# A 4-row transpose of softmax weights, widened to a transpose of a whole 128x128 tile that is zero but for those rows

## Chip, cores and metric

The kernel runs on one core of one Trainium2 chip. The metric is device time in microseconds; lower is better. Three runs of the kernel before gave 2450.37, 2450.66 and 2451.76 us, so the median is 2450.66 us. A profile of a further execution, with a record for every instruction, is what "the profile" and "the trace" mean below.

## The reference

There are 128 graphs of 128 nodes with 512 features each, and a weighted 128x128 adjacency matrix per graph, all in float32. Four layers follow one another, each of the form x = layernorm(x + layer(x, adj)). Layers 0, 2 and 3 multiply by a normalised adjacency and by weights. The change lies in layer 1, cut here to what matters:

```python
def _L1_gnn_ref(x, adj_matrix, W_qk, W_v):
    qk = jnp.einsum('bnd,ed->bne', x, W_qk)
    q, k = jnp.split(qk, 2, axis=-1)
    v = jnp.einsum('bnd,ed->bne', x, W_v)
    inv_scale = 1.0 / ATT_DIM ** 0.5
    scores = jnp.einsum('bnd,bmd->bnm', q, k) * inv_scale
    w = jnp.sum(scores * adj_matrix, axis=-1, keepdims=True)
    w = jax.nn.softmax(w, axis=1)
    return w * v
```

So each graph has one number w per node; these 128 numbers go through a softmax over the nodes, and row n of v is scaled by the weight of node n.

## The kernel before, in words

**Tiling.** The work is cut into 32 tiles of 4 graphs (G = 4, NT = 32). Nodes lie on the 128 partitions. A tile's features are a 128x4x512 array in SBUF (`x`), and everything of the four layers happens to it on chip. The tiles are staggered: in the loop at the end of the kernel function, one pass works on layers 0 and 1 of tile t and on layers 2 and 3 of tile u = t - 1, so that the matmuls of one can be placed among those of the other.

**Matmuls.** The layers' weight products use a 2x2 block scheme with seven products (B11, T1, B21, B22, T2, T3, T4), in `project` (line 526) for layers 0, 2 and 3 and in `l1_out` (line 729) for layer 1. Their results are the PSUM tiles `p_o` and `p_v` of the profile. A matmul of two float32 operands shows as two records in the trace; a transpose shows as one. Products of `project` take hooks: functions that are called after the product named, so that their TensorE instructions stand at that place in TensorE's order. GpSimd forms the sums of left operands (`agg3s` and the like), ScalarE copies PSUM to SBUF and normalises, VectorE adds results and takes the statistics.

**Softmax of layer 1.** `l1_scores` (line 695) leaves `w`, 128 nodes by 4 graphs. `l1_softmax` (line 716) transposes it on TensorE to 4 rows of 128 (PSUM tile `p_w`), takes each row's minimum on VectorE (the sign is turned, so this is the maximum of the scores), has ScalarE form the exponentials `e` with their sum, and has VectorE scale `e` in place by the reciprocal of the sum. `e` is a tile of 4 partitions by 128, of a tag with one buffer. `l1_add` (line 775) transposes `e` back to 128 nodes by 4 graphs on TensorE (PSUM tile `p_ws`), has VectorE copy that to `ws`, and then adds `v` scaled by `ws` to `x`. In TensorE's order `p_w` comes after product B11 of layer 3 of the tile before, and `p_ws` after its product B21 (line 903), so that four matmuls of B11, one transpose, four of T1, four of B21, the other transpose and four of T2 follow one another; in the trace, each four are eight records.

A TensorE transpose is a matmul whose stationary operand is the data and whose moving operand is the identity. The shapes in the profile name both: in `4*128 4x4`, the data has 4 rows and 128 columns and the identity is 4x4.

**What sets the order.** Every instruction is first recorded in a plan (class `Plan`, line 127). TensorE keeps the order in which the program recorded it. The other engines' instructions are ordered by a list scheduler (`schedule`, line 197): each has an estimated duration (`estimate`, line 292) and a due time worked back from those that need it. For a transpose on TensorE the estimate is

```python
max(109, 0.85 * n) if method == "transpose"
```

with n the number of elements of the output per partition. `emit` (line 268) then issues all instructions, which is why nearly every row of the profile names line 271; the tiles tell them apart. The PSUM tiles `p_w`, `p_ws`, `p_agg` and `p_xT` share a pool of three banks (`ps_t`, line 339) in turn. Constants such as `ident` (the identity) and `nhalf` (line 388) are made once at the start, from a pool of their own.

Of the kernel before, what the change touches and what calls it, by code (L numbers as in the profile page):

```python
# [10 lines left out]
FP = mybir.dt.float32  # L11
# [4 lines left out]
P = 128  # L16
K = 32
Q = P // K
G = 4
# [292 lines left out]
def kernel(  # L312
# [13 lines left out]
    nc = Plan(tc.nc, estimate)  # L326
# [4 lines left out]
    const = Pool(nc, ctx.enter_context(tc.tile_pool(name="const", bufs=1)), 1)  # L331
# [3 lines left out]
    sp = Pool(nc, ctx.enter_context(tc.tile_pool(name="sp", bufs=4)), 4)  # L335
# [7 lines left out]
    st = {}  # L343
# [15 lines left out]
    def weight(src, name, queue, turned=False):  # L359


        w = const.tile([P, 2, 7, H], FP, tag=name, name=name)
        for h in range(2):
            to = w[:, :, 2 * h:2 * h + 2].rearrange("p c j m -> p c (j m)")
            if turned:
                for b in range(Q):
                    queue.dma_start(to[b * K:(b + 1) * K], src.rearrange("(b h c k) m -> h b k c m", b=Q, h=2, c=2)[h][b])
            else:
                queue.dma_start(to, src.rearrange("(h c p) m -> h p c m", h=2, c=2)[h])
        return w  # L370
# [7 lines left out]
    def broadcast_row(src, name, queue):  # L378
        r = const.tile([P, F], FP, tag=name, name=name)
        queue.dma_start(r, bass.AP(tensor=src.tensor, offset=src.offset, ap=[[0, P], [1, F]]))  # L380
        return r

    ident = const.tile([P, P], FP, tag="ident", name="ident")
    make_identity(tc.nc, ident.real())
    p = ps_t.tile([P, C, P], FP, tag="pt", name="p_warm")
    for _ in range(WARM):
        nc.tensor.transpose(p[:, 0], ident, ident)
    nhalf = const.tile([P, G], FP, tag="nhalf", name="nhalf")
    nc.vector.memset(nhalf, -0.5)
    w0_sb = weight(w0, "w0_sb", nc.sync)  # L390
    b0_sb = broadcast_row(b0, "b0_sb", nc.sync)
    wqk_sb = tp.tile([P, C, 2 * ATT], FP, tag="row", name="wqk_sb", bufs=1)
# [233 lines left out]
    def norm_stats(name, t, r, pairs):  # L626
        if name == "o3" and (t, r, pairs[-1]) != (last, 1, 1):
            return norm_last(name, t, r, pairs)
        z = st["x", t]
        qs = slice(pairs[0], pairs[-1] + 1)  # L630
        mv = sp.tile([P, 2, 2], FP, tag="mv", name=f"mv{name}_{t}_{r}")
        for q in pairs:
            n = 2 if name == "o3" else 1
            s = sp.tile([P, n, 6], FP, tag="bn", name=f"bn{name}_{t}_{r}_{q}")
            for h in reversed(range(n)):
                nc.vector.bn_stats(s[:, h], z[:, 2 * q + r, h * (F // n):(h + 1) * (F // n)])
            nc.vector.bn_aggr(mv[:, q, :], s)
        rstd = sp.tile([P, 2], FP, tag="rstd", name=f"rstd{name}_{t}_{r}")
        mr = sp.tile([P, 2], FP, tag="mr", name=f"mr{name}_{t}_{r}")
        nmr = sp.tile([P, 2], FP, tag="nmr", name=f"nmr{name}_{t}_{r}")  # L640
        nc.gpsimd.tensor_scalar(rstd[:, qs], mv[:, qs, 1], LN_EPS, None, ALU.add)
        nc.gpsimd.tensor_tensor(rstd[:, qs], rstd[:, qs], nhalf[:, qs], ALU.pow)
        if name == "o3":
            zg = z[:, G - 1]
            nc.vector.tensor_scalar(zg, zg, mv[:, 1, 0:1], rstd[:, 1:2], ALU.subtract, ALU.mult)
            nc.sync.dma_start(out[B - 1], zg)
            return
        nc.gpsimd.tensor_tensor(mr[:, qs], mv[:, qs, 0], rstd[:, qs], ALU.mult)
        nc.scalar.mul(nmr[:, qs], mr[:, qs], -1.0)
        for q in pairs:  # L650
            zg = z[:, 2 * q + r, :]
            nc.scalar.activation(zg, zg, AF.Identity, bias=nmr[:, q:q + 1], scale=rstd[:, q:q + 1])
# [63 lines left out]
    def l1_softmax(t):  # L716
        p = ps_t.tile([P, P], FP, tag="pt", name=f"p_w_{t}")
        nc.tensor.transpose(p[:G, :], st.pop(("w", t)), ident)
        mn = sp.tile([G, 1], FP, tag="mn", name=f"mn_{t}")
        nc.vector.tensor_reduce(mn, p[:G, :], AX.X, ALU.min)  # L720
        e = sp.tile([G, P], FP, tag="e", name=f"e_{t}", bufs=1)
        ssum = sp.tile([G, 1], FP, tag="ssum", name=f"ssum_{t}")
        nc.scalar.activation(e, p[:G, :], AF.Exp, bias=mn, scale=-1.0, accum_out=ssum)
        rsum = sp.tile([G, 1], FP, tag="rsum", name=f"rsum_{t}")
        nc.vector.reciprocal(rsum, ssum)
        nc.vector.tensor_scalar(e, e, rsum, None, ALU.mult)
        st["e", t] = e

    def l1_out(t, hooks):

# [44 lines left out]
    def l1_add(t):  # L775

        p = ps_t.tile([P, P], FP, tag="pt", name=f"p_ws_{t}")
        nc.tensor.transpose(p[:, :G], st.pop(("e", t)), ident[:G, :G])
        ws = sp.tile([P, G], FP, tag="ws", name=f"ws_{t}")
        nc.vector.tensor_copy(ws, p[:, :G])  # L780
        for r in range(2):
            for g in (r, 2 + r):
                for h in range(2):
                    zg = st["x", t][:, g, h * H:(h + 1) * H]
                    nc.vector.scalar_tensor_tensor(zg, st["v", t][r, h][:, g // 2, 0:H], ws[:, g:g + 1], zg,
                                                   ALU.mult, ALU.add)
            norm_stats("v", t, r, (0, 1))
# [68 lines left out]
    def begin():  # L856

        prep_rows(0)
        prep_transpose(0)
        weight_sums(w0_sb, nc.vector)  # L860
        l0_agg(0, nc.vector, ONE_BY_ONE)
        prep_rows(1)
        l0_out(0, {B11: [lambda: prep_transpose(1)], B22: [lambda: l0_agg(1)]})
        weight_sums(wv_sb, nc.vector)
        for w in (w2x_sb, w2a_sb, w3_sb):
            weight_sums(w, nc.gpsimd)

        l0_out(1)
        l1_turn(0, turn_on_tensor, (0,))
        finish_tails()  # L870
        l1_turn(0, turn_on_tensor, (1,))
        l1_out(0, {T3: [lambda: l1_turn(1, turn_on_tensor)]})
        l1_out(1, {B11: [lambda: l1_scores(0)], T1: [lambda: l1_softmax(0)], B21: [lambda: l1_add(0)]})
        l2_both(0, 0)
        l2_out(0, {B11: [lambda: l2_both(0, 1), lambda: prep(2)], T1: [lambda: l1_scores(1)], T2: [lambda: l1_softmax(1)], T3: [lambda: l1_add(1)]})
        l0_agg(2)
        l2_turn(1)
        l0_out(2, {B21: [lambda: l2_agg(1, 0)], T1: [lambda: l2_agg(1, 1)]})
        l3_agg(0)
        l3_bias(0)  # L880
        l3_out(0)
# [8 lines left out]
    for t in range(2, NT):  # L890
        u = t - 1
        if t > 2:
            l0_out(t, {T1: [lambda: l2_agg(u, 0)], T2: [lambda: l2_agg(u, 1)]})
        tails.append(lambda: l1_turn(t))
        prep(t + 1)
        l2_out(u)
        if t < last:
            l0_agg(t + 1)
        l1_out(t, {})
        l3_agg(u)  # L900
        l1_scores(t)
        l3_bias(u)
        l3_out(u, {B11: [lambda: l1_softmax(t)], B21: [lambda: l1_add(t)]})
        if t < last:
            l2_turn(t)
# [43 lines left out]
```

## Time and profile before

| What | us |
|---|---|
| Median of three runs | 2450.66 |
| The profiled execution, its own time | 2451.53 |
| Its span, first to last instruction | 2449.8 |
| TensorE matmuls busy | 2437.9 |
| TensorE weight loads busy | 2087.3 |
| VectorE busy | 1714.5 |
| GpSimd busy | 1316.0 |
| ScalarE busy | 996.4 |

The mean granted TensorE clock of that execution is 0.999 of full speed. In the profile, PE is TensorE's matmuls, PEld its weight loads (they run beside the matmuls), DVE is VectorE, ACT is ScalarE, POOL is GpSimd and SP issues most DMAs. A row of groups reads: line, engine, operation, output<-inputs, shapes, count | busy time in us, mean ns of one | idle time of the engine just ahead of them, and what ended it. A row of the timeline reads: start in us, length in us, engine, line, operation, output<-inputs, shapes, count; instructions of one kind in succession are merged. Matmuls are pipelined, and the end of a record is modelled, so records overlap. "issue" means that the engine waited for nothing that the profile shows.

### The profile page before, as it was taken

To read this page: it belongs to the slowest core of one execution; us is meant where nothing else is said; L and a number is where in the kernel's file an instruction comes from. 1 tells how busy PE (TensorE), PEld (TensorE's weight loads), DVE (VectorE), ACT (ScalarE), POOL (GpSimd) and SP (SyncE) were. 2 spreads that over 40 slices of the span, in tenths; PEclk is the share of its full clock that TensorE was granted. 3 is DMA by queue.
4 is the path that set the end of the run, shared out by engine and by line. 5 is a ranking of instruction groups with operands and counts; after the bars stand their busy time and mean duration, and the time that the engine had idled before them with its cause. 6 is when DMAs were issued, how large, how long until landed. Compare 5 with 4: busy or idle time off the path is not lost.

```text
span 2449.8 us, 35470 instructions
## 1 busy us (share of the span) xinstructions
PE 2437.9 (100%) x12462; PEld 2087.3 (85%) x12462; DVE 1714.5 (70%) x3396; ACT 996.4 (41%) x2117; POOL 1316.0 (54%) x1580
## 2 busy tenths in 40 slices
PE   9999999999999999999999999999999999999998
PEld 7888888888888888888888888888888888888887
DVE  7767766677666777766776667766677676777666
ACT  4334343443434444344443444333444334443345
POOL 6464555555555555555455554645546455555543
PEclk9999999999999999999999999999999999999999
DMA  5133233442424423244332443234442333423220
GB/s 181 48 99 104 73 108 91 125 125 57 116 78 125 125 69 109 78 121 125 84 93 82 117 125 104 73 99 104 120 125 61 96 102 117 125 74 96 67 80 35
DMA packets 393266, 241.15 MB, mean 98 GB/s; under 512 B 140416, under 2 KB 358016, under 8 KB 393088
## 3 DMA queue, kind: packets, MB, share of 16 engines
q1 hardware_dynamic: 393088, 238.88, 35.4%
q8 instruction: 99, 1.62, 0.3%
q14 instruction: 79, 0.65, 0.1%
HBM read 126.62 MB, written 112.20 MB: 97 GB/s over the span
## 4 chain that ended last, share of the span: by engine, by line
PE 96%; DMA 1%; DVE 1%; POOL 1%; SPq 0%; issue 0%; ACT 0%; POOLq 0%; DVEq 0%
PE p_o L271 61%; PE p_v L271 20%; PE p_agg L271 14%; PE p_sc L271 1%; SPq L271 0%; DMA x<-in_x_dram 0%; PE p_w L271 0%; DVE x L271 0%; DMA xT1s<-x 0%; DVE u_o L271 0%; PE p_ws L271 0%; DMA xT1y<-xT1s 0%; PE p_xT L271 0%; POOL xT2s L271 0%; DMA xT2y<-xT2s 0%
## 5 line engine op out<-in xcount | busy, mean ns | idle before, releaser
L271 PE MATMUL p_o<-w_sb,agg 128*128 128x256 f32 x2048 | 471.3, 380 | 0.9 <-DVE u_o L271 0.9
L271 PEld LDWEIGHTS p_o<-w_sb,agg 128*128 128x128 f32 x2048 | 386.1, 190 | 52.8 <-DVE u_o L271 0.9
L271 ACT COPY agg<-p_agg 128x512 f32<-128x512 f32 (+1 forms) x415 | 226.3, 553 | 406.0 <-PE p_agg L271 405.8
L271 PE MATMUL p_v<-wv_sb,xT 128*128 128x320 f32 x1024 | 291.7, 433 | 0.1
L271 PE MATMUL p_o<-w2x_sb,xT 128*128 128x256 f32 x1024 | 263.0, 379 | 1.0 <-ACT xT L271 1.0
L271 DVE TENSOR_TENSOR v<-p_v,v 128x320 f32<-128x320 f32 x316 | 154.5, 490 | 155.4 <-PE p_v L271 154.8
L271 PE MATMUL p_o<-w2a_sb,agg 128*128 128x256 f32 x1024 | 262.8, 379 | 0.0
L271 PEld LDWEIGHTS p_v<-wv_sb,xT 128*128 128x128 f32 x1024 | 191.9, 190 | 76.7 <-ACT xT L271 0.6
L271 PEld LDWEIGHTS p_agg<-anT,x 128*128 128x128 f32 x2048 | 238.7, 192 | 7.0 <-DVE anT L271 0.5
L271 DVE TENSOR_TENSOR u_o<-p_o,u_o 128x512 f32<-128x512 f32 (+1 forms) x196 | 129.1, 671 | 160.6 <-PE p_o L271 159.1
L271 PE MATMUL p_agg<-anT,x 128*128 128x128 f32 x2048 | 239.4, 275 | 0.3 <-DVE anT L271 0.3
L271 PEld LDWEIGHTS p_o<-w2x_sb,xT 128*128 128x128 f32 x1024 | 194.2, 190 | 30.8 <-ACT xT L271 1.4
L271 PE MATMUL p_v<-wv_sb,xT1s 128*128 128x320 f32 x768 | 217.6, 433 | 0.8 <-POOL xT1s L271 0.6
L271 PEld LDWEIGHTS p_o<-w2a_sb,agg 128*128 128x128 f32 x1024 | 194.6, 190 | 26.4
L271 POOL TENSOR_SCALAR rstdo<-mvo 128x2 f32<-128x2 f32 (+1 forms) x131 | 35.7, 272 | 320.9 <-DVE mvo L271 318.3
L271 PE MATMUL p_o<-w2x_sb,xT2s 128*128 128x256 f32 x768 | 197.2, 379 | 0.0
L271 PE MATMUL p_o<-w2a_sb,agg2s 128*128 128x256 f32 x768 | 197.1, 379 | 0.0
L271 ACT ACTIVATE x<-x,nmro,rstdo 128x512 f32<-128x512 f32 x256 | 195.0, 808 | 3.4
L271 PEld LDWEIGHTS p_v<-wv_sb,xT1s 128*128 128x128 f32 x768 | 145.5, 190 | 59.0 <-POOL xT1s L271 2.0
L271 PE MATMUL p_o<-w_sb,agg0s 128*128 128x256 f32 x768 | 181.1, 379 | 0.4 <-DVE u_o L271 0.4
L271 PE MATMUL p_o<-w_sb,agg3s 128*128 128x256 f32 x744 | 173.8, 383 | 0.0
L271 DVE BATCH_NORM_STATS2 bno<-x 128x6 f32<-128x512 f32 x258 | 170.4, 682 | 3.9
(146 smaller groups left out, 4255.8 us busy)
## 6 DMA issues: line engine op xcount, KB each, us to landing
x<-in_x_dram SPq DMA_DIRECT2D x31, 1024.0 KB, 6.5
out_dram<-x SPq DMA_DIRECT2D x31, 1024.0 KB, 5.4
xT2s<-x SPq DMA_DIRECT2D x120, 256.0 KB, 2.8
xT2y<-xT2s SPq DMA_DIRECT2D x240, 128.0 KB, 2.7
xT1s<-x SPq DMA_DIRECT2D x120, 256.0 KB, 2.5
xT1y<-xT1s SPq DMA_DIRECT2D x240, 128.0 KB, 3.1
sa<-ana SPq DMA_DIRECT2D x120, 128.0 KB, 3.2
ya<-sa SPq DMA_DIRECT2D x120, 128.0 KB, 3.3
```

Source lines behind the costliest of these rows:

```text
L271: getattr(getattr(self.nc, op.engine), method)(*[v.real() if isinstance(v, Ref) else v for v in args], **{k: v.real() if isinstance(v, Ref ...
```

## The change

A constant tile `e_sb` of 128x128 is made at the start and filled with zeros by VectorE. In `l1_softmax`, `e` is no longer a tile of its own but rows 0 to 3 of `e_sb`; the exponentials are written and scaled there, and rows 4 to 127 stay zero. In `l1_add`, the transpose takes the whole of `e_sb` as data and the whole identity, and writes all 128 columns of `p_ws`. Columns 0 to 3 hold what they held before, and only those are copied to `ws`; columns 4 to 127 are zeros that nobody reads.

```diff
+    e_sb = const.tile([P, P], FP, tag="e_sb", name="e_sb")
+    nc.vector.memset(e_sb, 0.0)
...
-        e = sp.tile([G, P], FP, tag="e", name=f"e_{t}", bufs=1)
+        e = e_sb[:G, :]
...
-        st["e", t] = e
...
-        nc.tensor.transpose(p[:, :G], st.pop(("e", t)), ident[:G, :G])
+        nc.tensor.transpose(p, e_sb, ident)
```

## The prediction

> **What bounds the kernel now.** I read the page first: busy shares, then the chain of work that ended last.
>
> ```profile
> span 2449.8 us, 35470 instructions
> PE 2437.9 (100%) x12462; PEld 2087.3 (85%) x12462; DVE 1714.5 (70%) x3396; ACT 996.4 (41%) x2117; POOL 1316.0 (54%) x1580
> ...
> PE 96%; DMA 1%; DVE 1%; POOL 1%; SPq 0%; issue 0%; ACT 0%; POOLq 0%; DVEq 0%
> ```
>
> TensorE is busy for the whole span and is 96% of the chain, so a nanosecond of TensorE time is a nanosecond of the kernel, and nothing else counts unless it makes TensorE wait. But a busy PE hides what a matmul really costs: the records overlap, since each is drawn longer than the distance to the next. The cost must be read from start to start. Next I took the small transposes by tile, among the groups with shapes kept apart (matmuls, then weight loads).
>
> ```profile
> L271 PE MATMUL p_w<-ident,w 128*4 128x128 f32 x32 | 8.6, 270 | 0.1
> L271 PE MATMUL p_ws<-ident,e 4*128 4x4 f32 x32 | 7.0, 220 | 0.0
> ...
> L271 PEld LDWEIGHTS p_ws<-ident,e 4*128 4x128 f32 x32 | 4.3, 133 | 10.7 <-issue 10.7
> ```
>
> p_ws is the transpose that the change edits: 32 of them, one per tile, 0.22 us each, and 10.7 us of weight-load idle that no semaphore explains (0.33 each). Last, TensorE alone in time, in the last tile but for its end:
>
> ```profile
> 2383.65 0.59 PE L271 MATMUL p_o<-w_sb,agg 128*128 128x256 f32 x2
> 2384.08 0.27 PE L271 MATMUL p_w<-ident,w 128*4 128x128 f32 x1
> 2384.19 1.89 PE L271 MATMUL p_o<-w_sb,agg3s 128*128 128x256 f32 x8
> 2385.92 1.89 PE L271 MATMUL p_o<-w_sb,agg 128*128 128x256 f32 x8
> 2387.74 0.22 PE L271 MATMUL p_ws<-ident,e 4*128 4x4 f32 x1
> 2387.89 3.29 PE L271 MATMUL p_o<-w_sb,agg3s 128*128 128x256 f32 x14
> ```
>
> One p_o record is 0.38 us; eight in a row take 1.89, so their starts lie (1.89 - 0.38) / 7 = 0.216 apart. The last of the eight before p_ws thus starts at 2385.92 + 7 x 0.216 = 2387.43. From there: p_ws starts 0.31 later (0.216 is the streaming of that p_o; 0.094 is idle array), the next p_o starts 0.15 after p_ws, and the 14 that follow take 3.29 where 13 x 0.216 + 0.38 = 3.19: another 0.10 at the first of them. Taking p_ws out would leave one step of 0.216, so it costs 0.310 + 0.150 + 0.104 - 0.216 = 0.348 us. (The third decimal is from the starts in the trace; all 32 p_ws show it within 2 ns, also the two with other neighbours.) The same view gives the price of p_w, a transpose that streams 128 columns from all 128 rows: it starts 2384.08 - (2383.65 + 0.59 - 0.38) = 0.22 after the p_o before it, the next p_o starts 0.11 later, and that one's eight take 1.89, so no gap on either side. It costs 0.109 us.
>
> **What the Trainium skill says.** "TensorEngine Tiling (Array Packing)", section Key Properties, says that changing the tiling mode drains TensorE; its list of configurations has modes of 32 rows, which is what a 4-row operand would fit. The trace agrees in kind: p_ws, the only matmul with fewer than 128 rows, is the only one with a gap on both sides, and p_w, with 4 columns but all rows, has none where its operand is ready. "TensorE: Matmul & The Clock Gate", section Step-by-step, says that the next tile's weights load while this one's matmul runs, pulled ahead where row groups do not conflict or the load goes to the background buffer. The trace agrees: the load of a p_o starts with the matmul before it, that of p_ws only at 2387.74, with its own matmul. The same page's LDWEIGHTS section says that load time goes by columns, not rows: 133 ns for the 4-row load, 141 for a 128-row one (p_xT), so the full tile loads about as fast.
>
> **The change part by part.** The instruction lists of the two kernels, compared engine by engine with numbers and line shifts taken off, have the same order. The planner's estimate for a transpose is max(109, 0.85 x columns), which is 109 for 4 and for 128, so no due time moves; only the points below differ.
>
> 1. p_ws from 4 to 128 rows (both operands) and from 4 to 128 streamed columns. The nearest rows are p_w (128 rows, 128 columns, 0.109) and p_xT (128x128 weights too; eight in a row take 1.04 with a record of 0.272, so (1.04 - 0.272) / 7 = 0.110 each). I take 0.109. Saved: 0.348 - 0.109 = 0.239 per tile, x 32 = 7.65 us, all on the bounding engine. Bounds: if only one of the two gaps goes, about 0.1 less per tile (4.4 us left); if neither goes, see the slower rival.
>
> 2. The e that p_ws waits for. In every other tile the scaling of e ends late. At 1860.51 it lasts 1.10, end 1861.61; the last p_o before that p_ws starts at 1860.19 + 7 x 0.216 = 1861.70. From DVE's end to TensorE's load the trace shows 0.11 (p_w waits so: last DVE end 1933.84, load 1933.95). So the load of e, now free to run under that p_o, starts at 1861.72 and has until 1861.92. It needs 0.11 at the steady pace, 0.19 as the longest record: just covered. I take 0; if the cover fails, up to 0.1 in 14 tiles, 1.4 us. A gain is excluded, as nobody waits for e alone.
>
> 3. 31 matmuls (p_agg of layer 2, two p_xT) now also wait for TensorE's own semaphore, since p_ws fills as much of the bank as its successor in it. The p_ws meant is 18 lines of the list back, some 12 us, so the count is long reached. A semaphore instruction takes 51 ns on TensorE's queue, which runs ahead: p_agg rows with such waits show 0.0 idle. I take 0; bound 31 x 0.05 = 1.6 us; no gain.
>
> 4. The memset of e_sb, once, on DVE: the nearest row is GpSimd's memset of the same size, 0.20 us. After its first memset (end 0.85) DVE sits idle for 2.73 us until adj lands at 3.58. Cost 0; uncovered, 0.2 us once.
>
> 5. e shares one buffer over tiles as before (a tag with one buffer), so Exp waits for no one new; Exp, reduce and scaling have the same 4x128 shape.
>
> What is late next when TensorE runs 0.239 ahead? After p_ws it needs GpSimd's agg3s (done before p_ws) and DVE's reads of two regions. DVE sits idle 0.31 us for TensorE at 1864.19 in that tile, 0.65 in the neighbour (1939.82): more than 0.239, so DVE moves along with TensorE and each later wait keeps its distance. p_w's own wait (0.145 in 28 tiles) is behind DVE's queue, and that queue too is tied to TensorE by then; it stays.
>
> Sum: span 2449.8 - 7.65 = 2442.1. That execution took 2451.53, which is 1.73 outside the span: 2443.9 for its like. The median of the runs shown, 2450.66, lies 0.87 below that execution, so I forecast 2450.66 - 7.65 = 2443.0.
>
> **The rivals.**
> A. Part of it comes back: the load of e is late in every other tile (1.4 us), or the semaphore waits show (1.6), or one of both gaps stays. For it: a cover of only 0.1 us. Against: no p_agg is late now with two waits. With the first two, 2446.0; 2444.5 with one.
> B. The gaps come from the hand-over (a wait on two semaphores in mid-stream), not from the rows: the change does nothing for them, and streaming is free under them: 2450.7. Against: p_w has the same two waits, and at 2384.08 no gap.
> C. Slower. The gaps stay, and the stream now has 128 columns in place of 4: 0.109 x 124 / 128 = 0.105 more per tile, x 32 = 3.4 us: 2454.0. The place is p_ws on TensorE; it decides if p_ws still starts 0.31 after the p_o before it. For it: the stationary operand still has 128 columns and the change widens all else. Against: p_xT, of the very shape, follows others at 0.109 with no gap.
>
> **How the numbers follow.** Forecast case (2442.2 to 2444.0) 0.80; A 0.11, which ends at 2446.2 with both waits shown in full; B 0.05; C 0.04. The bound of what can be told from no change is 0.2%, 4.9 us, that is 2445.8: A lies mostly under it. Faster 0.89, same 0.07, slower 0.04. The range runs from 2442.0 (half the spread of the three runs under the forecast case) to 2446.2; it leaves out B and C, 0.09.
>
> **What would show it.** p_ws as 128*128 128x128, near 272 ns, its load near 141 and without the idle for issue; the start of p_ws 0.216 after the p_o before, the next p_o 0.11 after it, and eight p_o in 1.89 behind that. Memset of e_sb before 1.2 us; chain still 96% PE; span near 2442. Wrong, if p_ws starts 0.31 after its p_o (C or B), if "DVE e" appears ahead of p_ws among the waits (A), or if TensorE's gaps are gone and the span is not shorter: then DVE held TensorE elsewhere.

## The result and the profile after

The changed kernel takes 2445.07 us (median of 10 runs, 2443.5 to 2446.01), the kernel before 2451.32 (10 runs, 2450.37 to 2452.36). The ratio is 0.9973, with a 95% interval of 0.9965 to 0.9981: faster by 4.7 to 8.6 us, 6.25 between the medians. A second measurement, among the experiments, gave 7.45.

The page of the changed kernel has the same picture as before: span, busy time by engine, and the chain by engine.

```profile
span 2443.3 us, 35474 instructions
...
PE 2430.7 (99%) x12462; PEld 2088.2 (85%) x12462; DVE 1714.2 (70%) x3397; ACT 996.3 (41%) x2117; POOL 1318.7 (54%) x1580
...
PE 97%; DVE 1%; POOL 0%; DMA 0%; issue 0%; ACT 0%; SPq 0%; POOLq 0%; DVEq 0%
```

The small transposes among the changed kernel's groups, matmuls and then the weight load:

```profile
L271 PE MATMUL p_ws<-ident,e_sb 128*128 128x128 f32 x32 | 8.7, 272 | 0.0
...
L271 PEld LDWEIGHTS p_ws<-ident,e_sb 128*128 128x128 f32 x32 | 4.5, 140 | 1.3
```

The records of p_ws have become longer in sum, 8.7 us of matmul for 7.0 and 4.5 of loads for 4.3, and the kernel is faster. What went is the idle of the load for "issue", 10.7 us before and not in the row now. TensorE in time, in the last tile but for its end, shows it from start to start:

```profile
2377.66 0.27 PE L271 MATMUL p_w<-ident,w 128*4 128x128 f32 x1
2377.76 1.89 PE L271 MATMUL p_o<-w_sb,agg3s 128*128 128x256 f32 x8
2379.49 1.89 PE L271 MATMUL p_o<-w_sb,agg 128*128 128x256 f32 x8
2381.22 0.27 PE L271 MATMUL p_ws<-ident,e_sb 128*128 128x128 f32 x1
2381.33 3.19 PE L271 MATMUL p_o<-w_sb,agg3s 128*128 128x256 f32 x14
```

The last of the eight p_o before p_ws starts at 2379.49 + 7 x 0.216 = 2381.00. p_ws starts 0.22 later, the next p_o 0.11 after that, and its fourteen take 3.19, which is 13 x 0.216 + 0.38 with nothing over. All three gaps are gone. By the starts in the trace, all 32 p_ws cost 0.111 us or within 2 ns of it (two have other neighbours), against 0.348 before: 0.237 saved per tile, 7.6 us in all.

The weight loads around p_ws show what the gaps are made of. Before:

```profile
2387.74 0.13 PEld L271 LDWEIGHTS p_ws<-ident,e 4*128 4x128 f32 x1 [0.33 <-issue]
2387.89 0.30 PEld L271 LDWEIGHTS p_o<-w_sb,agg3s 128*128 128x128 f32 x2
```

and in the changed kernel:

```profile
2381.01 0.14 PEld L271 LDWEIGHTS p_ws<-ident,e_sb 128*128 128x128 f32 x1
2381.22 0.30 PEld L271 LDWEIGHTS p_o<-w_sb,agg3s 128*128 128x128 f32 x2
```

Before, the load of p_ws and that of the p_o behind it begin with their own matmuls (2387.74 and 2387.89). In the changed kernel they begin 0.21 and 0.11 ahead of them, under the matmul before. The second p_o load follows the first by 0.11, since one lasts 0.19 and the two together 0.30; the gap of 0.104 behind p_ws is of that size. So of the 0.348, only the 0.094 ahead is a wait before anything of p_ws begins, and much of the rest is two loads that no matmul covers.

This execution's span is shorter by 6.5, not by 7.6. The rest lies in the first 24 us. TensorE there, before:

```profile
1.34 5.74 PE L271 MATMUL p_warm<-ident 128*128 128x128 f32 x30 [1.34 <-POOL ident masks.py:199]
...
20.36 1.99 PE L271 MATMUL p_o<-w_sb,agg0s 128*128 128x256 f32 x8 [0.35 <-DVE u_o L271]
22.19 2.06 PE L271 MATMUL p_agg<-anT,x 128*128 128x128 f32 x17
```

and in the changed kernel:

```profile
1.35 6.20 PE L271 MATMUL p_warm<-ident 128*128 128x128 f32 x30 [1.35 <-POOL ident masks.py:199]
...
21.38 1.99 PE L271 MATMUL p_o<-w_sb,agg0s 128*128 128x256 f32 x8 [0.81 <-DVE u_o L271]
23.21 1.05 PE L271 MATMUL p_agg<-anT,x 128*128 128x128 f32 x8
```

The warm-up transposes, the same 30 in both, took 0.46 us longer, and by 23 us the kernel is 1.0 late. By the starts in the traces, p_warm goes at first at 0.213 us from start to start and then at 0.109; the pace changes after 21 steps before and after 26 in the changed kernel, which accounts for the 0.46. Another 0.46 is the longer wait of p_o for u_o. Whether the new memset does that is the first question for the experiments.

### The profile page after: what moved, and what is told of

It reads as the page before. It is cut to its first block, busy times and chain, and to the rows that moved or that the text cites. A ratio compares the mean times of both kernels' runs of the same rounds, so it can differ in the third digit from the quotient of the medians.

```text
span 2443.3 us, 35474 instructions
## 1 busy us (share of the span) xinstructions
PE 2430.7 (99%) x12462; PEld 2088.2 (85%) x12462; DVE 1714.2 (70%) x3397; ACT 996.3 (41%) x2117; POOL 1318.7 (54%) x1580
## 4 chain that ended last, share of the span: by engine, by line
PE 97%; DVE 1%; POOL 0%; DMA 0%; issue 0%; ACT 0%; SPq 0%; POOLq 0%; DVEq 0%
PE p_o L271 62%; PE p_v L271 20%; PE p_agg L271 14%; PE p_sc L271 1%; DMA ana<-in_adj_dram 0%; PE p_w L271 0%; DVE x L271 0%; DVE u_o L271 0%; PE p_xT L271 0%; PE p_ws L271 0%; DVE w_sb L271 0%; DVE ana L271 0%; DVE agg0s L271 0%; POOL rstdo L271 0%; POOL w2x_sb L271 0%
```

## The experiments

The theory: a matmul with few rows among matmuls of 128 rows empties TensorE on both sides, so rows are what counts. The rivals: the stream of 4 columns is too short to cover the weight loads; or the transpose mode does it. The two other transposes vary rows and columns together; the three matmuls vary them one at a time. By the traces, p_ws has the same two semaphore waits in all of these kernels, so the hand-over, rival B of the prediction, is no difference between them. In the table, the steps are ns from start to start as most tiles have them: into p_ws, between its two records where it has two, from p_ws to the next p_o, and from that p_o to its successor. The cost is their sum less two steps of 216. The last columns hold 32 times the cost less that of the kernel before, and what was measured.

| p_ws | rows x streamed columns | steps | cost, us | worked out, us | measured, us |
|---|---|---|---|---|---|
| before, transpose | 4 x 4 | 310, 150, 320 | 0.348 | - | - |
| rows64, transpose | 64 x 64 | 310, 202, 320 | 0.400 | +1.7 | +1.75 |
| rows96, transpose | 96 x 96 | 216, 87, 242 | 0.113 | -7.5 | -6.86 |
| changed, transpose | 128 x 128 | 216, 109, 218 | 0.111 | -7.6 | -6.25, -7.45 |
| mm_r4c4, matmul | 4 x 4 | 309, 132, 178, 320 | 0.507 | +5.1 | +5.63 |
| mm_r4c128, matmul | 4 x 128 | 309, 213, 200, 320 | 0.610 | +8.4 | +8.98 |
| mm_r128c4, matmul | 128 x 4 | 216, 28, 112, 299 | 0.223 | -4.0 | -3.67 |

Every measured value lies above the one worked out, by 0.1 to 1.3 us, and each interval (1.6 to 3.8 us either way) covers the one worked out. A small cost that these kernels share, outside p_ws, is thus neither shown nor excluded.

**The memset alone.** The kernel before, with this added:

```diff
+    e_sb = const.tile([P, P], FP, tag="e_sb", name="e_sb")
+    nc.vector.memset(e_sb, 0.0)
```

> The kernel before with only the memset of a 128x128 tile of zeros added at the start; e and its transpose stay 4 rows. Theory (the 1.1 us that the changed kernel lost in its first 24 us is chance of the start, a later grant of the clock): time within 0.7 us of the kernel before, p_ws at 0.31 / 0.15 / 0.10 as before. Rival (the memset, or what moves in SBUF with it, delays the start): about 1.1 us slower, with the wait of p_o for DVE u_o near 20 us at 0.8 in place of 0.35.

2451.55 us beside 2451.70 for the kernel before, ratio 0.9999 (0.9991 to 1.0008); the gaps at p_ws are there. The memset in its trace, by tile (count, then min, median and max in ns):

```profile
L271 DVE MEMSET e_sb<- x1: 165/165/165, 0.8 to 0.8; 128x128 f32 x1
```

TensorE in time has the wait that the rival named, but not the delay:

```profile
20.66 1.99 PE L271 MATMUL p_o<-w_sb,agg0s 128*128 128x256 f32 x8 [0.80 <-DVE u_o L271]
22.49 1.72 PE L271 MATMUL p_agg<-anT,x 128*128 128x128 f32 x14
```

p_agg starts at 22.49: 0.3 after the kernel before, 0.7 ahead of the changed one. So in this execution the memset brings a third of the loss at most; the interval of the time, 2 us either way, is too wide to tell 1.1. That called for the kernel before, profiled again.

> The kernel before, profiled once more, for its first 24 us. Theory (the start varies by chance): the second block of p_o from agg0s, which started at 20.36 in its first profile and between 20.47 and 21.38 in kernels with the memset, starts 0.1 us or more off 20.36. Rival (the memset sets it): again at 20.36 within 0.05, with a wait of 0.35.

```profile
20.01 1.99 PE L271 MATMUL p_o<-w_sb,agg0s 128*128 128x256 f32 x8 [0.35 <-DVE u_o L271]
21.84 2.39 PE L271 MATMUL p_agg<-anT,x 128*128 128x128 f32 x20
```

The same program is 0.35 earlier at this place than in its first profile, with the wait the rival named and the start that it did not. The pace of p_warm changes after 16 steps here, where it was 21. The span is 2449.8 all the same. So a start early by a third of a microsecond is chance and need not reach the end. The expectation left out two kernels with the memset: in rows64 and in the version called later, both below, this block starts at 20.36 and 19.86. Over ten profiles with the memset it starts between 19.86 and 21.38, and over two without it at 20.01 and 20.36. The ranges overlap; a share of the memset of a few tenths of a microsecond remains open.

**The changed kernel once more,** unaltered, beside the others:

> The changed kernel itself once more, beside the others. Theory (all 7.6 us that the trace shows at p_ws are gained; the first measurement's 6.25 fell short by chance of the start): ratio near 0.9969, 7 to 8 us faster than before. Rival (about 1.3 us are given back in every run): ratio near 0.9974, 6.0 to 6.5 us faster.

2444.42 us beside 2451.87: 7.45 faster, ratio 0.9971 (0.9959 to 0.9982), span 2442.6. TensorE in time, where it was 1.0 late in its first profile:

```profile
20.47 1.99 PE L271 MATMUL p_o<-w_sb,agg0s 128*128 128x256 f32 x8 [0.57 <-DVE u_o L271]
```

The same program starts this block 0.91 earlier than in its first profile, and the pace of p_warm changes after 16 steps in place of 26. So the late start belongs to that one execution, not to the change. At p_ws the steps are the same in both profiles. The interval covers both expectations, and the median sides with the first. That all of the first ten executions fell short by chance of the start is not shown, as only one of them was profiled.

**Rows.** In place of the whole tile:

```diff
-        nc.tensor.transpose(p, e_sb, ident)
+        nc.tensor.transpose(p[:, :64], e_sb[:64], ident[:64, :64])
```

> The changed kernel, but the transpose takes 64 rows of e_sb and a 64x64 identity, so p_ws has 64*128 64x64. Theory (fewer rows than the whole array put TensorE into another tiling, with an idle array on both sides): p_ws again starts 0.31 after the p_o before it, costs 0.35 to 0.40, the time is that of the kernel before, 0 to +1.7 us. Rival (it was the short stream of 4 columns that could not cover the loads): the gaps are gone or half gone, p_ws costs about 0.11 to 0.2, 5 to 7 us faster than before.

2453.45 us beside 2451.70, ratio 1.0008 (0.9999 to 1.0016). TensorE in time, last tile but for its end:

```profile
2387.25 1.89 PE L271 MATMUL p_o<-w_sb,agg 128*128 128x256 f32 x8
2389.07 0.27 PE L271 MATMUL p_ws<-ident,e_sb 64*128 64x64 f32 x1
2389.27 3.07 PE L271 MATMUL p_o<-w_sb,agg3s 128*128 128x256 f32 x13
```

2389.07 is 0.31 after the last p_o's start (2387.25 + 7 x 0.216 = 2388.76): the gap of 4 rows, unchanged with 64 rows and a stream sixteen times as long. The step after it grew by 52 ns. Next, the same edit with 96:

> The changed kernel, but the transpose takes 96 rows of e_sb and a 96x96 identity: p_ws is 96*128 96x96. Theory (a matmul of 96 rows already has the whole array, as the skill's list of tilings ends at 64 rows): no gaps, p_ws costs about 0.11, 7 to 8 us faster than before. Rival (every matmul with fewer than 128 rows has the gaps): p_ws starts 0.31 after the p_o before it and costs 0.40 to 0.43, 1.6 to 2.6 us slower.

2445.01 us beside 2451.87, ratio 0.9972 (0.9961 to 0.9982).

```profile
2379.45 1.89 PE L271 MATMUL p_o<-w_sb,agg 128*128 128x256 f32 x8
2381.18 0.25 PE L271 MATMUL p_ws<-ident,e_sb 96*128 96x96 f32 x1
2381.27 3.00 PE L271 MATMUL p_o<-w_sb,agg3s 128*128 128x256 f32 x13
```

No gap ahead: 2381.18 is 0.22 after the start before it. The edge lies between 64 and 96 rows, and "fewer than 128" is ruled out. The change needed no more than 96 rows.

**Stream and mode.** The transpose as an ordinary float32 matmul, which is two records, with its estimate in the plan held at 109 so that the order of all instructions stays:

```diff
-        nc.tensor.transpose(p, e_sb, ident)
+        nc.tensor.matmul(p[:, :G], e_sb[:G], ident[:G, :G], start=True, stop=True)
```

> The changed kernel, but p_ws is an ordinary float32 matmul of 4 rows of e_sb with a 4x4 identity (two records in place of one); its estimate in the plan is held at 109, so the order is unchanged. Base for the two like it. Theory (rows): gaps as before ahead of the first and behind the second record, cost about 0.35 plus a second load of 0.11 to 0.15, so 0.46 to 0.5 per tile, 3.5 to 5 us slower than before. Rival (it is the transpose mode with 4 rows that drains): no gap of 0.31, cost about 0.22, 4 us faster than before.

2457.33 us beside 2451.70, ratio 1.0023 (1.0013 to 1.0033): 5.6 us slower at a cost of 0.507, both a little above what the theory expected.

```profile
2391.63 1.89 PE L271 MATMUL p_o<-w_sb,agg 128*128 128x256 f32 x8
2393.45 0.38 PE L271 MATMUL p_ws<-ident,e_sb 4*128 4x4 f32 x2
2393.76 3.07 PE L271 MATMUL p_o<-w_sb,agg3s 128*128 128x256 f32 x13
```

The gap of 0.31 is there without the transpose mode. With all rows, `e_sb` and `ident[:, :G]`:

> As the ordinary matmul of 4 rows, but with all 128 rows of e_sb and 4 columns of the identity, so 128*128 128x4: only the rows differ. Theory (rows): no gap ahead of it, only the loads show: 0.11 for each of two records, 0.22 per tile, 4 us faster than before. Rival (the short stream): the cost of the 4-row matmul, 0.46 to 0.5, 3.5 to 5 us slower than before.

2448.03 us beside 2451.70, ratio 0.9985 (0.9978 to 0.9991).

```profile
2382.06 1.89 PE L271 MATMUL p_o<-w_sb,agg 128*128 128x256 f32 x8
2383.79 0.28 PE L271 MATMUL p_ws<-ident,e_sb 128*128 128x4 f32 x2
2383.93 3.05 PE L271 MATMUL p_o<-w_sb,agg3s 128*128 128x256 f32 x13
```

The stream is as short as before and the gap is gone (2383.79 is 0.22 after 2383.57). What a short stream does cost shows here alone: the steps 28, 112 and 299 are two loads of about 0.11 that 4 columns do not cover, 0.223 in sum. And with 4 rows but all columns, `e_sb[:G]` and `ident[:G, :]`:

> The ordinary matmul of 4 rows, but with 128 columns of the identity streamed in place of 4: only the length of the stream differs. Theory (rows): the gap of 0.31 ahead and 0.10 behind stay, and two streams of 128 columns come on top of the cost of 0.507 that the 4-column one showed: 0.6 to 0.72 per tile, 8 to 12 us slower than before. Rival (a long stream covers the loads and the gaps): about 0.22 per tile, 4 us faster than before.

2460.85 us beside 2451.87, ratio 1.0039 (1.0023 to 1.0054).

```profile
2394.24 1.89 PE L271 MATMUL p_o<-w_sb,agg 128*128 128x256 f32 x8
2396.06 0.48 PE L271 MATMUL p_ws<-ident,e_sb 4*128 4x128 f32 x2
```

The last p_o starts at 2394.24 + 7 x 0.216 = 2395.75, so the gap of 0.31 ahead stays, and 320 behind with it, whatever the stream. The three together leave the rows as the one factor, of those tried, that makes the gaps.

**Beyond the change.** In the changed kernel p_w still waits for w. Moving both hooks one product on:

```diff
-        l3_out(u, {B11: [lambda: l1_softmax(t)], B21: [lambda: l1_add(t)]})
+        l3_out(u, {T1: [lambda: l1_softmax(t)], T2: [lambda: l1_add(t)]})
```

> The changed kernel with both transposes of the softmax one product later in the steady passes: the hook of p_w behind T1 in place of B11, that of p_ws behind T2 in place of B21. In the changed kernel p_w starts 0.36 after the p_o before it in 28 tiles, 0.145 of it a wait for w behind DVE's queue, 4 us in all. Theory (the wait is only DVE being a little late, and what follows p_ws has slack): p_w's gap falls to 0.216, 4 us faster than the changed kernel, 11 to 12 us faster than before. Rival (the additions to x come 1.7 us later, and a later wait, of p_o or p_agg for x or its sums, takes it back): no faster than the changed kernel.

2445.25 us beside 2451.87, ratio 0.9972 (0.9961 to 0.9982): no faster than the changed kernel, which took 2444.42 beside the same 2451.87. The wait of p_w did go; the idle of its load fell from 10.5 us to 0.9. TensorE in time after the last p_ws has what came for it:

```profile
2379.63 1.24 PE L271 MATMUL p_o<-w_sb,agg3s 128*128 128x256 f32 x5
2383.18 3.65 PE L271 MATMUL p_o<-w_sb,agg 128*128 128x256 f32 x8 [2.31 <-DVE u_o L271]
```

In the last tile no other tile's matmuls stand behind p_ws, and TensorE stands still for 2.31 us, 0.59 in the changed kernel. So the last tile was put back:

```diff
+        at = (T1, T2) if t < last else (B11, B21)
+        l3_out(u, {at[0]: [lambda: l1_softmax(t)], at[1]: [lambda: l1_add(t)]})
```

> The version with both softmax transposes one product later, but for the last tile, which keeps B11 and B21. The one before it removed the wait of p_w (4.5 us in sum) and lost 3 us behind the last p_ws, where p_o waits for DVE u_o 2.3 us in place of 0.6, as no other tile's work stands there. Theory: with the last tile at its old place the loss is gone, about 4 us faster than the changed kernel, 11 to 12 us faster than before (ratio near 0.9953). Rival (the loss comes from all tiles adding up to a shift that shows at the end, whatever the last tile does): time as that version, 7 us faster than before.

2443.28 us beside 2451.68, ratio 0.9964 (0.9951 to 0.9978): 8.4 faster than before, one more than the changed kernel's 7.45, and their intervals overlap, so the two are not told apart. The theory's 4 us failed. The loss in the last tile is gone, but among the waits between 120 and 2300 us two are larger than in the changed kernel, where the first is absent and the second is 0.4 us once:

```profile
PEld p_o L271 <- POOL xT2s L271: 1.9, 3, 0.9
PEld p_v L271 <- POOL xT1s L271: 1.3, 3, 0.6
```

So part of the 4.5 us that p_w waited comes back as waits for sums that GpSimd forms from turned x, in a few tiles; that they are late because the additions to x are later is argued, not tried.

## Why the prediction was right

The mechanism was right: the gaps at p_ws went, at the price forecast. The time was right with some luck. 2445.07 lies inside the range, but outside the forecast case (2442.2 to 2444.0, given 0.80) and in the part that the range kept for rival A. None of A's causes shows in the trace (points 2 and 3, and all gaps went). So the width that held the result was there for another reason. Point by point, by its steps:

1. **p_ws: right, to 2 ns.** 0.239 per tile was forecast from p_w and p_xT, 0.237 is measured. All three gaps went, so rivals B and C (gaps that stay) are out; rows64 shows what C would have looked like, at 64 rows.
2. **The cover of e: right, and as thin as worked out.** In a tile with the late e, VectorE's scaling in the changed kernel is

```profile
1855.89 1.10 DVE L271 TENSOR_SCALAR e_sb<-e_sb,rsum 4x128 f32<-4x128 f32 x1
```

and TensorE is

```profile
1855.56 1.89 PE L271 MATMUL p_o<-w_sb,agg 128*128 128x256 f32 x8
1857.29 0.27 PE L271 MATMUL p_ws<-ident,e_sb 128*128 128x128 f32 x1
```

e is done at 1856.99, 0.08 before the last p_o starts at 1857.07, and p_ws follows that after 0.22. In 14 tiles with the late e, the load of p_ws begins about 0.03 later after the start of that p_o than in the others, 0.116 after the end of e (0.11 was forecast), but no p_ws starts later for it.

3. **The waits on TensorE's own semaphore: right.** By the starts in both traces, p_agg comes 0.216 after the p_o ahead of it, on the mean of 96 such places, with and without them.
4. **The memset: right in the main.** It takes 0.165 for the 0.20 taken, from 0.85 us, and VectorE then idles 2.50 us until adj lands. A share of a few tenths of a microsecond in the start is not excluded.
5. **What is late next: right.** p_w's wait stays, 4.2 us over 28 tiles before and 4.5 after, 0.2 of the difference in one tile; nothing behind p_ws became late.

The sum was 7.65 and the first measurement 6.25. Of the 2.07 us between 2443.0 and 2445.07, 0.66 is the base (the kernel before is 2451.32 over ten runs, 2450.66 over the three it rested on), and 1.4 is the saving, of which the profiled execution shows 1.0 in its first 24 us. The prediction gave no term to the chance of the start; whether that is also what the other nine executions lost stays open. The second measurement, 7.45, has most of it back. The ends of its range are not quite what its terms give: half the spread under 2443.0 is 2442.3, not 2442.0, and both waits of A in full end at 2446.0, not 2446.2. Neither decides anything here.

The drain that "TensorEngine Tiling (Array Packing)", section Key Properties, names fits: gaps at 4 and 64 rows, none at 96 and 128, as its section Tiling Modes has 64 rows as the largest below 128 (the list that the expectation for 96 rows meant). The runs show the edge and the price, and that a good part of the price is two weight loads left uncovered; that the cause is a change of tiling is the page's word.

## What to carry to other kernels

Read a matmul's price from start to start, up to the second matmul behind it: the record of p_ws was 0.22 us, its cost 0.348, and after the change 0.27 and 0.111. In a stream of 128-row matmuls a lone one with 4 or with 64 rows cost more than a full one (0.348 and 0.400 against 0.111); padding its operand with zeros to 96 or 128 rows costs one memset when the rows stay zero. Moving an operand's use later removes its own wait, but the last tile, with nothing behind it, has to be looked at apart.

## What was not expected of the hardware

The edge lies between 64 and 96 rows, with the same 0.094 us ahead for 4 and for 64 rows. The load of a 4-row or 64-row p_ws, and that of the 128-row p_o behind it, begin with their own matmuls in all 32 tiles; with 96 and 128 rows they begin ahead. This also sets the two records of the 4-row matmul 132 ns apart, against 28 with 128 rows and the same 4 columns: the first load begins with the first record and the second load 108 ns later, while with 128 rows the first load begins about 0.2 us ahead. And a padded 96-row transpose streams in 87 ns but leaves the next load 26 uncovered (242 in place of 216), so that it costs what 128 rows cost.
